# Group 1's input in four 8-row tiles, 16 rows of group 0 scaled on GpSimd, and coefficients three steps later

## Chip, core and metric

The kernel runs on one NeuronCore of one Trainium2 chip. The metric is the device time of one execution in microseconds; the median of three runs is given. Engines are named as in the profile: PE (TensorE, PEld its weight loads), DVE (VectorE), ACT (ScalarE), POOL (GpSimd) and SP (SyncE, which here only issues DMAs; SPq is its queue).

## What is computed

The input x has shape (32, 48, 64, 128): batch, channels, height, width, in fp32. Two layers of the same form are applied:

```
x = x + scan(groupnorm(x, 16 groups), weights of layer 0)
x = x + scan(groupnorm(x, 16 groups), weights of layer 1)

step:   nxt = inp + conv1d(carry, w, K=5 over the line, 48 -> 48 channels) + b
down:   over the rows 0..63, carry = the row above
up:     over the rows 62..0, same weights
right:  over the columns 0..127, right weights
left:   over the columns 126..0, left weights
```

Group normalization takes mean and variance over 3 channels x 64 x 128 of each image, with eps 1e-5 and no learned factors. Every scan step needs the one before it.

## The kernel before

**Groups and phases.** The batch is cut into four groups of 8 images (0 to 3). `PHASES` is the order of work: rows of group 0, rows of group 1, columns of groups 0 and 1 together, then rows of group 2, rows of layer 1, and so on: 12 phases. A row phase has 126 steps (63 down, 63 up), a column phase 254. A step (`step`, line 647) is nine matmuls into three PSUM tiles (line 658) and three VectorE additions of PSUM, bias and input, in place in SBUF (line 667). Steps are counted through the whole kernel: step 0 is the first of group 0's rows, step 126 the first of group 1's.

**Layout.** For a row phase the 64 rows of a group lie in two of three SBUF slots, half of the rows in each; a slot is six units of 128 x 2048. `arena` holds the three slots and four more units, `stage`. The channels and eight columns share the partitions, in three blocks (o = 0, 1, 2).

**How a group gets in.** `plan_input` plans it for groups 1 to 3. `take_in` loads rows of x into a tile (`nat`), half of the rows on partitions 0 to 47 and half on 64 to 111. In the kernel before, group 1's tiles hold 16 rows and there are two (`nats1`), which take turns over four loads; a tile of 8 rows or more per half is loaded image by image with `take_batch`, 192 KB each. `permute` (line 499, GpSimd) reorders a tile into two 8 KB-per-partition tiles in `stage`, 16 copies for each 8 rows. `put_out` stores them to the DRAM tensor `xin`, in DMAs of 384 KB. `take_others` makes the statistics on ScalarE: for each image and each 512 elements a sum (line 364), a negation for all of them together (line 372), and a sum of squares about the mean (line 356). `scaling`, spread over the steps by `spread` at one piece a step, turns them into scale and offset for each channel and image; its first VectorE instructions are lines 382 (needs the sums) and 387 (needs the squares). It ends with `coeffs`, 14 steps after its start.

**How rows get into a scan.** `plan_rows` plans, by step, `move_rows` (loads `xin` into the slots, or stores results to `upa`; 10 DMAs for 8 rows and 20 for 16, in pieces of 128 bytes) and `scale_rows` (ScalarE applies scale and offset in place, line 542, 24 activations for each call). `scale_at_once` (line 546) does the same with two tensor_tensor operations on an engine of choice (line 553); before, only VectorE used it, for group 0's rows 0 to 3. Group 0 is fed by `first_group`, written out by hand; its rows 40 to 63 are scaled by `scale_rows` at steps 10, 26 and 32.

**What sets the order.** `at(t, ...)` puts a call on an agenda for step t; the agenda is sorted and emitted between the steps. `in_order` keeps the emitted order on every engine and queue. A planned step is thus a place in each engine's program, not a time: an engine or a queue can run ahead of the steps or behind them. Within one engine nothing overtakes: a VectorE instruction that waits holds up all the additions behind it, and a DMA on SP's queue that waits holds up every later one. Each DMA also waits for the DMA eight places before it.

The places around the change: group 1's row loads at steps 92, 108, 128 and 144 (`ahead`), its scaling at 112, 124, 143 and 159 (`scaled`), the stores of group 0's rows 56 to 63 at 94, then 8 rows each at 102, 110 and 118.

Of the kernel before, what the change touches and what calls it, by code (L numbers as in the profile page):

```python
# [91 lines left out]
def kernel(  # L92
# [8 lines left out]
    nc = tc.nc  # L101
# [8 lines left out]
    UNIT = NH * LINE  # L110
    SLOT = 2 * NG * UNIT
# [147 lines left out]
    def stat_tile(shape, name, key):  # L259
        return stat_pool.tile(shape, F32, tag=name, name=f"{name}_{key}")  # L260

    def scaling(key, layer, g, averages, masks):


        n = len(masks)
        yield from averages(key)
        mean_p, var_p = averages.result

        def average(ps, rhs):
            for i in range(n):  # L270
                nc.tensor.matmul(ps, masks[i], rhs[:, i], start=i == 0, stop=i == n - 1)

        def expand(ps, rhs):
            for o in range(NG):
                nc.tensor.matmul(ps[:, o], maskp[:, o], rhs, start=True, stop=True)

        def small(name):
            return stat_tile([FULL, NG, GB], name, key)

        ps = ps_stat.tile([FULL, 2 * NG + 2, GB], F32, tag="ps_stat", name=f"ps_{key}")  # L280
        average(ps[0:P, 0], mean_p)
        yield
        mean_c = stat_tile([P, GB], "mean_c", key)
        nc.vector.tensor_copy(mean_c, ps[0:P, 0])
        yield
        expand(ps[:, 1 : 1 + NG], mean_c)
        yield
        mean = small("mean")
        nc.vector.tensor_copy(mean, ps[:, 1 : 1 + NG])
        at = mean if n > 1 else mean_c.unsqueeze(1)  # L290
        np_ = FULL if n > 1 else P
        spare = small("dev")
        dev = spare[0:np_, 0:n]
        nc.vector.tensor_tensor(dev, mean_p, at, ALU.subtract)
        nc.vector.tensor_tensor(dev, dev, dev, ALU.mult)
        nc.vector.tensor_tensor(dev, dev, var_p, ALU.add)
        yield
        average(ps[0:P, 1 + NG], dev)
        yield
        var_c = stat_tile([P, GB], "var_c", key)  # L300
        nc.vector.tensor_copy(var_c, ps[0:P, 1 + NG])
        yield
        expand(ps[:, 2 + NG :], var_c)
        yield
        var = small("var")
        nc.vector.tensor_scalar(var, ps[:, 2 + NG :], GN_EPS, None, ALU.add)

        std = small("std")
        nc.scalar.activation(std, var, AF.Sqrt)
        yield  # L310
        yield
        r0 = std
        nc.vector.reciprocal(r0, std)
        t0 = spare
        nc.vector.tensor_tensor(t0, var, r0, ALU.mult)
        nc.vector.tensor_tensor(t0, t0, r0, ALU.mult)
        yield
        nc.vector.tensor_scalar(t0, t0, -0.5, 1.5, ALU.mult, ALU.add)
        scale, offset = (
            stat_pool.tile(  # L320
                [FULL, NG, GB], F32, tag=f"{t}{layer}{g}", name=f"{t}{layer}{g}"
            )
            for t in ("scale", "offset")
        )
        nc.vector.tensor_tensor(scale, r0, t0, ALU.mult)
        nc.vector.scalar_tensor_tensor(offset, mean, -1.0, scale, ALU.mult, ALU.mult)
        coeffs[layer, g] = scale, offset
# [140 lines left out]
    x_masks = [mask_sb]  # L468
# [45 lines left out]
    def row(k, h):  # L514
        return row_views(k)[h // HALF][:, :, h % HALF]
# [221 lines left out]
    def at(t, fn, *args):  # L737
        agenda.append((t, len(agenda), fn, args))

    def spread(t, gen, every):  # L740


        def go(t):
            if next(gen, "end") != "end":
                at(t + every, go, t + every)
                agenda.sort(key=lambda a: a[:2])

        at(t, go, t)

    def plan_input(g, times, work, lag, nats, perms):  # L750

        stats = InputStats(f"x{g}", 0)
        rows = nats[0].shape[-1] // W
        ahead, pieces_of = len(nats), rows * W // BN
        per = rows * W * GB // perms[0].shape[-1]
        for j, t in enumerate(times):
            nat = nats[j % ahead]
            if j == 0 and g > 1:
                at(t - 7, take_in, g, 0, nat)
            for i in range(per):  # L760
                perm, r = perms[i % len(perms)], i * rows // per
                at(t + i * work / per, permute, nat, r, perm, [nc.gpsimd])
                at(t + i * work / per + 4, put_out, g, 2 * rows * j + r, perm, rows)
            at(t + lag, stats.take_others, pieces_of * j, nat)
            if j + ahead < len(times):
                free = t + (13.5 if g == 1 else 7)
                at(free, take_in, g, 2 * rows * (j + ahead), nat)
        spread(t + work + lag + (0, 3, 8, 5)[g], scaling(f"x{g}", 0, g, stats, x_masks), 1)

    def plan_rows(k, t0, prev):  # L770
        if k == 1:
            ahead, scaled = (-34, -18, 2, 18), (-14, -2, 17, 33)
        elif prev == "cols":
            ahead, scaled = (-28, -12, 4, 20), (-13, 3, 19, 35)
        else:
            ahead, scaled = (-54, -43, 0, 11), (-22, -8, 16, 30)
        if k:
            for i in range(4):
                at(t0 + ahead[i], move_rows, k, i * LOAD, (i + 1) * LOAD, False)
                at(t0 + scaled[i], scale_rows, k, i * LOAD, (i + 1) * LOAD)  # L780

        cuts = list(range(0, H + 1, E8))
        following = PHASES[k + 1][0] == "cols"
        if following and follows(k + 1):
            cuts = [0, E8 // 4] + cuts[1:]
        for h0, h1 in zip(cuts, cuts[1:]):
            t = t0 + 2 * (H - 1) - h0
            if k == 0:
                t += 24 if h0 >= HALF else 68
            elif not following:  # L790
                t = t0 + 92 + 5 * (H - h1) / E8 + (34 if h1 <= HALF else 0)
            at(t, move_rows, k, h0, h1, True)
        at(
            t0 + H - 1,
            nc.gpsimd.tensor_copy,
            last.rearrange("p (o n) -> p o n", o=NG),
            row(k, H - 1),
        )

    def follows(k):  # L800

        _, layer, pair = PHASES[k]
        return PHASES[k - 1] == ("rows", layer, 2 * pair + 1)
# [104 lines left out]
    starts = [0]  # L908
# [5 lines left out]
    def wide_nat(i0, n):  # L914
        return arena[0:P, i0 : i0 + GB * n * W].rearrange("p (b m) -> p b m", b=GB)

    tiles = [stage[0:P, i] for i in range(4)]
    nats1 = [wide_nat(2 * SLOT + i * UNIT * 4, 8) for i in range(2)]
    plan_input(1, [starts[0] + 38 + 13 * j for j in range(4)], 11, 2, nats1, tiles[2:4])
    nats = [wide_nat(3 * SLOT, 4)]  # L920
    times = [starts[2] + 16 + 13.5 * j for j in range(8)]
    plan_input(2, times, 6, 6, nats, tiles[2:4])
    times = [t + 15 * j for t in (starts[3] + 42, starts[4] + 24) for j in range(4)]
    plan_input(3, times, 6, 7, nats, tiles[2:4])

    def more_weights(key, layer, way):
# [135 lines left out]

    in_order(first_group)
    at(starts[0] + 10, scale_rows, 0, 40, 48)
    at(starts[0] + 22, take_in, 1, 16, nats1[1])
    at(starts[0] + 26, scale_rows, 0, 48, 56)
    at(starts[0] + 32, scale_rows, 0, 56, 64)

    agenda.sort(key=lambda a: a[:2])
    done = 0  # L1070
# [65 lines left out]
```

## Time and profile before

| what | value |
|---|---|
| median of three runs | 4380.13 us (4379.56 to 4392.25) |
| profiled execution | 4375.56 us, span of the core 4373.8 us |
| mean granted TensorE clock | 0.98 |
| busy: PE / DVE / ACT / POOL | 95% / 49% / 31% / 19% |
| loads of x for group 1 | 64 DMAs of 192 KB |
| loads of x for groups 2 and 3 | 32 DMAs of 768 KB, median 12.1 us from issue to landing |
| stores to `xin` for groups 1 to 3 | 96 DMAs of 384 KB, median 5.5 us |

Times in a timeline are us from the span's start; a line gives start, length, engine, source line, operation, out<-in, number of merged instructions, and in brackets the idle time before it and what ended that. The span is the profiled core's own time; the execution's time is 1.8 us longer. A busy share is an average over the whole span, so it says little about a single stage.

### The profile page before, as it was taken

Reading aid. Unit: us, or ns where it says so; the run is one execution under the profiler, and the core shown is the slowest. Engines: PE = TensorE matmul, PEld = TensorE weight load, DVE = VectorE, ACT = ScalarE, POOL = GpSimd, SP = SyncE. Lnnn points to the kernel's source line nnn. Section 1 sums busy time; section 2 is a strip of 40 time slices with the busy share of each in tenths; the row PEclk is TensorE's granted clock in tenths of the full one; section 3 lists DMA queues with packets and bytes.
Section 4 is the critical chain, followed back from the end, with each engine's and each line's share of the span. In section 5 each row is a group of like instructions: output and inputs, shape, how many; then the busy total and the mean of one; then the engine's idle time right before and its main releaser. Section 6 shows DMA issues by size and latency. Waiting matters only on the chain. (4 is left out here: it accounts for less than half of the span.)

```text
span 4373.8 us, 90099 instructions
## 1 busy us (share of the span) xinstructions
PE 4149.4 (95%) x36632; PEld 4120.7 (94%) x36632; DVE 2164.2 (49%) x6558; ACT 1360.7 (31%) x2698; POOL 820.4 (19%) x775
## 2 busy tenths in 40 slices
PE   5889997999999999998999999999999999999992
PEld 2889997999999999998999999999999999999992
DVE  6344443456665444443446665444444444444443
ACT  2783301434785554100005774503000002110122
POOL 4351000324332020000004310000000024510352
PEclk9999998999999999999999999999999999999996
DMA  9989789866999989579407989939188039989999
GB/s 194 176 171 154 116 149 183 225 120 189 235 195 147 155 156 158 99 124 209 77 1 222 224 174 143 134 51 165 35 141 189 1 76 240 245 239 159 168 196 182
DMA packets 2111167, 680.34 MB, mean 156 GB/s; under 512 B 2000928, under 2 KB 2053920, under 8 KB 2070816
## 3 DMA queue, kind: packets, MB, share of 16 engines
q1 hardware_dynamic: 2010496, 576.00, 69.7%
q10 hardware_dynamic: 100256, 98.59, 10.8%
q8 instruction: 288, 4.72, 0.5%
q14 instruction: 127, 1.04, 0.1%
HBM read 397.57 MB, written 295.98 MB: 159 GB/s over the span
## 5 line engine op out<-in xcount | busy, mean ns | idle before, releaser
L542 ACT ACTIVATE arena<-arena,offset,scale 128x256 f32<-128x256 f32 (+2 forms) x864 | 601.2, 790 | 412.4 <-DVE arena L667 142.4
L595 POOL TENSOR_TENSOR arena<-arena 128x2048 f32<-128x2048 f32 x80 | 363.0, 4553 | 1660.0 <-PE step_01l L658 504.4
L499 POOL COPY arena<-arena 112x256 f32<-112x256 f32 x458 | 270.3, 646 | 753.7 <-DMA arena<-in_x 504.1
L433 ACT ACTIVATE early<-arena 128x256 f32<-128x256 f32 x192 | 129.5, 675 | 687.5 <-DMA arena<-xin 547.4
L658 PE MATMUL step_00r<-arena,early 128*128 128x128 f32 x2286 | 258.6, 277 | 22.6 <-DMA arena<-upa 22.6
L658 PEld LDWEIGHTS step_00r<-arena,early 128*128 128x128 f32 x2286 | 258.4, 194 | 22.9 <-issue 22.8
L658 PE MATMUL step_01r<-arena,early 128*128 128x128 f32 x2286 | 257.4, 276 | 20.1 <-DMA arena<-upa 20.1
L658 PEld LDWEIGHTS step_01r<-arena,early 128*128 128x128 f32 x2286 | 257.1, 193 | 20.4 <-issue 20.3
L364 ACT ACTIVATE early<-arena 112x512 f32<-112x512 f32 x192 | 121.0, 630 | 460.5 <-PE step_00r L658 246.6
L658 PE MATMUL step_11r<-arena,early 128*128 128x128 f32 x2286 | 258.9, 277 | 3.9 <-DVE arena L667 3.9
L658 PEld LDWEIGHTS step_11r<-arena,early 128*128 128x128 f32 x2286 | 258.2, 193 | 4.4 <-DVE arena L667 4.2
L658 PE MATMUL step_00l<-arena,wleft 128*128 128x128 f32 x2286 | 256.3, 275 | 0.0
L658 PE MATMUL step_10r<-arena,early 128*128 128x128 f32 x2286 | 256.0, 275 | 0.0
L658 PEld LDWEIGHTS step_10r<-arena,early 128*128 128x128 f32 x2286 | 255.7, 192 | 0.3
L658 PEld LDWEIGHTS step_00l<-arena,wleft 128*128 128x128 f32 x2286 | 255.7, 192 | 0.0
L658 PE MATMUL step_11l<-arena,wleft 128*128 128x128 f32 x2286 | 255.5, 275 | 0.0
L658 PE MATMUL step_10l<-arena,wleft 128*128 128x128 f32 x2286 | 255.5, 275 | 0.0
L658 PE MATMUL step_01l<-arena,wleft 128*128 128x128 f32 x2286 | 255.4, 275 | 0.0
L658 PEld LDWEIGHTS step_10l<-arena,wleft 128*128 128x128 f32 x2286 | 255.4, 192 | 0.0
L658 PEld LDWEIGHTS step_11l<-arena,wleft 128*128 128x128 f32 x2286 | 255.4, 192 | 0.0
L658 PEld LDWEIGHTS step_01l<-arena,wleft 128*128 128x128 f32 x2286 | 255.3, 192 | 0.0
L620 ACT COPY arena<-arena 128x256 f32<-128x256 f32 x172 | 99.5, 657 | 415.5 <-POOL arena L595 127.5
(175 smaller groups left out, 7043.9 us busy)
## 6 DMA issues: line engine op xcount, KB each, us to landing
xin<-arena SPq DMA_DIRECT2D x96, 384.0 KB, 5.5
arena<-xin SPq DMA_DIRECT2D x96, 384.0 KB, 8.1
mid<-arena SPq DMA_DIRECT2D x96, 384.0 KB, 7.8
arena<-mid SPq DMA_DIRECT2D x192, 192.0 KB, 4.4
upb<-arena SPq DMA_DIRECT2D x192, 192.0 KB, 3.9
arena<-upb SPq DMA_DIRECT2D x96, 384.0 KB, 11.8
arena<-xin SPq DMA_DIRECT2D x186, 192.0 KB, 4.3
upa<-arena SPq DMA_DIRECT2D x180, 192.0 KB, 3.9
```

The lines of the kernel that those rows point to most:

```text
L364: nc.scalar.activation(junk[0:P], piece, AF.Identity, accum_out=self.sum[:, at[0], at[1]],)
L433: nc.scalar.activation(junk[:, 0:n], view[:, b], AF.Identity, accum_out=self.sum[:, i, j : j + 1])
L499: copy(dst[:, r, q], src[:, r0 + r, q])
L542: nc.scalar.activation(args[0], args[0], AF.Identity, bias=args[2], scale=args[1])
L595: eng.tensor_tensor(unit, unit, nat, ALU.add)
L620: copy(by_w(perm)[:, a], src[:, a])
L658: nc.tensor.matmul(part(whole(ps[o]), -s), weights[:, i, FULL * (o - NG * s - i + 1) : FULL * (o - NG * s - i + 2)], part(src(i), s), star ...
```

## The change

Group 1's input goes through four tiles of 8 rows in place of two of 16, in the same memory. With 4 rows per half, `take_in` uses its other branch: one DMA of 768 KB for each half in place of eight of 192 KB. The tiles are planned at steps 46, 52, ... 88 (before: 38, 51, 64, 77), each permuted over 5 steps, with statistics 1 step after; a tile is reloaded 7 steps after its start (before: 13.5). The first four loads are emitted at the end of `first_group` and at steps 23, 24 and 25; before, the second one was at step 22.

Rows 48 to 55 and 56 to 63 of group 0 are scaled by GpSimd with `scale_at_once`, at steps 26 and 33, in place of ScalarE at steps 26 and 32. On GpSimd these four operations stand between its last permute of group 0 and its first of group 1.

The start of group 1's `scaling` is last tile + work + lag + an extra: before 77 + 11 + 2 + 3 = 93, after 88 + 5 + 1 + 2 = 96. The scaling of group 1's first 16 rows moves from step 112 to 114.

On SP's queue the order after is: eight loads of x, then four times (four stores, two loads), then twelve stores, the loads of group 1's rows 0 to 15, and the last tile's four stores, two ahead of group 0's first eight result rows and two behind them. No stored, loaded or computed element is added or left out.

```diff
         def plan_input(g, times, work, lag, nats, perms):
             ...
             if j + ahead < len(times):
-                free = t + (13.5 if g == 1 else 7)
+                free = t + 7
                 at(free, take_in, g, 2 * rows * (j + ahead), nat)
-        spread(t + work + lag + (0, 3, 8, 5)[g], scaling(f"x{g}", 0, g, stats, x_masks), 1)
+        spread(t + work + lag + (0, 2, 8, 5)[g], scaling(f"x{g}", 0, g, stats, x_masks), 1)
 
     def plan_rows(k, t0, prev):
         if k == 1:
-            ahead, scaled = (-34, -18, 2, 18), (-14, -2, 17, 33)
+            ahead, scaled = (-34, -18, 2, 18), (-12, -2, 17, 33)
         ...
-    nats1 = [wide_nat(2 * SLOT + i * UNIT * 4, 8) for i in range(2)]
-    plan_input(1, [starts[0] + 38 + 13 * j for j in range(4)], 11, 2, nats1, tiles[2:4])
+    nats1 = [wide_nat(2 * SLOT + i * UNIT * 2, 4) for i in range(4)]
+    plan_input(1, [starts[0] + 46 + 6 * j for j in range(8)], 5, 1, nats1, tiles[2:4])
     ...
     in_order(first_group)
     at(starts[0] + 10, scale_rows, 0, 40, 48)
-    at(starts[0] + 22, take_in, 1, 16, nats1[1])
-    at(starts[0] + 26, scale_rows, 0, 48, 56)
-    at(starts[0] + 32, scale_rows, 0, 56, 64)
+    for j in range(1, 4):
+        at(starts[0] + 22 + j, take_in, 1, 8 * j, nats1[j])
+    at(starts[0] + 26, scale_at_once, 0, 48, 56, nc.gpsimd)
+    at(starts[0] + 33, scale_at_once, 0, 56, 64, nc.gpsimd)
```

## The prediction

> **What bounds the kernel now.** I read the page's table of busy time and its slices first, then windows, then the timelines of the engines in the windows with a hole.
>
> ```profile
> PE 4149.4 (95%) x36632; PEld 4120.7 (94%) x36632; DVE 2164.2 (49%) x6558; ACT 1360.7 (31%) x2698; POOL 820.4 (19%) x775
> PE   5889997999999999998999999999999999999992
> PEclk9999998999999999999999999999999999999996
> ```
>
> TensorE works 95% of the span. A slice is 109 us: after the first seven the row of digits is almost all 9. The 2,024 steps (eight row phases of 126, four column phases of 254) are a serial chain of nine matmuls and three VectorE additions, 2.015 us a step, that no part of the change touches. So a gain can only come from holes in the first 700 us. Windows of 10 us (columns: length, busy PE, PEld, DVE, ACT, POOL, granted clock, DMA share, GB/s) show the largest, and a smaller one later:
>
> ```profile
> 300.00:310.00 10.00, 9.03 (x81) 8.83 (x80) 3.84 (x12) 5.71 (x16) 0.00 (x0) 1.00 1.05 166
> 310.00:320.00 10.00, 2.23 (x10) 2.24 (x11) 2.03 (x6) 9.56 (x27) 5.50 (x10) 0.71 0.51 164
> 320.00:330.00 10.00, 1.55 (x10) 1.36 (x8) 0.07 (x1) 9.54 (x24) 8.68 (x16) 0.67 0.67 157
> 330.00:340.00 10.00, 8.63 (x63) 8.64 (x64) 5.68 (x18) 0.00 (x0) 8.80 (x16) 0.77 0.67 158
> 460.00:470.00 10.00, 2.94 (x19) 2.51 (x19) 1.03 (x3) 10.00 (x15) 0.00 (x0) 0.72 1.09 165
> ```
>
> ScalarE is full while TensorE stands. The VectorE timeline says what it stands for:
>
> ```profile
> 316.13 0.22 DVE L382 TENSOR_REDUCE mean_x_x<-sum_x_x 112x8 f32<-112x64 f32 x1 [8.73 <-ACT early L364]
> 329.93 0.55 DVE L387 TENSOR_TENSOR neg_x_x<-neg_x_x,mean_x_x 112x64 f32<-112x64 f32 x1 [11.70 <-ACT early L356]
> 468.19 0.35 DVE L667 SCALAR_TENSOR_TENSOR arena<-step_01d,bd,arena 128x128 f32<-128x128 f32 x1 [8.28 <-DMA arena<-xin]
> ```
>
> L382 and L387 compute group 1's coefficients. They stand in VectorE's program order ahead of the additions (L667) of steps 94 and 95, and wait for ScalarE's last sums (L364) and squares (L356). The third is row 32 of group 1's scan, waiting for its scaled input. TensorE's own idle there is 8.74, 9.81 and 7.06 us. What stands behind ScalarE and the DMAs is in the timelines of ScalarE, GpSimd and SP's queue:
>
> ```profile
> 169.29 48.01 ACT L542 ACTIVATE arena<-arena,offset,scale 128x128 f32<-128x128 f32 x94 [2.33 <-DMA arena<-xin]
> 220.52 9.42 POOL L499 COPY arena<-arena 112x256 f32<-112x256 f32 x16 [66.96 <-DMA arena<-in_x]
> 314.50 9.32 POOL L499 COPY arena<-arena 112x256 f32<-112x256 f32 x16 [16.35 <-DMA xin<-arena]
> 196.72 33.20 SPq L199 DMA_DIRECT2D arena<-in_x  x32
> 304.05 41.85 SPq L199 DMA_DIRECT2D xin<-arena  x16
> 345.99 22.36 SPq L199 DMA_DIRECT2D arena<-xin  x20
> 430.18 39.96 SPq L199 DMA_DIRECT2D arena<-xin  x40
> L595 POOL TENSOR_TENSOR arena<-arena 128x2048 f32<-128x2048 f32 x80 | 363.0, 4553 | 1660.0 <-PE step_01l L658 504.4
> ```
>
> ScalarE scales until 217.3 and only then takes statistics, 25.9 us per 16-row tile (16 sums at 0.755, one negation, 16 squares at 0.846). GpSimd is free from 153.6 to 220.5. SP needs 149.3 us (196.72 to 345.99) for group 1's pass. At the rates seen (loads of x at 165 GB/s, 12.6 MB; the stores at about 380 GB/s, 12.6 MB) it is 76 + 33 = 109 us; 40 us are waits between load, permute and store.
>
> **What the Trainium skill says.** "GPSIMD Engine Reference", Elementwise — side-by-side cycle accounting, gives 4497 ns for a GpSimd tensor_tensor of 2048 fp32; L595 above agrees with 4553. The same page, Specifications, says that the two engines share SBUF ports and contend when VectorE has two SBUF inputs. L667 has one and one from PSUM; its minimum, median and maximum here are 340, 350 and 354 ns, with GpSimd busy or not, so I charge nothing. "TensorE: Matmul & The Clock Gate", What's actually happening, says that idleness of some 3.4 us halves the clock until it has been busy as long. Here the clock is 0.67 to 0.77 around the holes, and the nine matmuls after one took 3.8 us instead of 2.0: a hole costs some 1.8 us beyond itself. "DMA: Bandwidth & Descriptors", Measured (HBM→SBUF), has larger transfers run faster. For x this trace doesn't: a 768 KB pair of group 2, alone, moved 143 to 244 GB/s between 872 and 879 us, no better than the 192 KB loads. I take 165 GB/s for both.
>
> **The change part by part.**
>
> Scaling on GpSimd. ScalarE loses 48 of its 168 128x128 activations (0.51 us each): free at 169.3 + 46 x 0.51 = 192.8. GpSimd gains four operations of 128 x 3072. At 4553/2048 = 2.22 ns per element each is 6.8 us, 13.7 for 8 rows. (VectorE's L553 with the same broadcast took 1.14 ns an element, its plain L595 1.12, so broadcasting is free there.) Rows 48 to 55 land at about 190.8 (SP issues them by 186.5, 4.3 us to landing): done at 204.5. Rows 56 to 63: done at 218.1. VectorE's last addition of the down scan is at 244.7, so they are needed at 214.5 and 230.6. Slack 10 and 12.5 us: no cost, while one operation stays under 10 us. Queued behind are GpSimd's permutes, which started at 220.5 anyway. Bounds: 5 us each (nothing gained) to 14 (16 us lost).
>
> Four tiles. SP issues eight loads at 196.7, as many bytes as before; after some 4 us of backlog a tile lands every 9.5 us: 210.5, 220, 229.5, 239. ScalarE needs 13.05 us a tile: 210.5 + 8 x 13.05 = 314.9, its last sums at 308. Tiles 4 to 7 must not starve it. SP's order is four stores, two loads, and so on. Tile 0's stores wait behind the loads and land at 243; from there load plus stores take 9.5 + 4.2 = 13.7: tiles 4 to 7 land at 253, 266, 280, 294, and ScalarE wants them at 263, 276, 289, 302. After that GpSimd's 4.7 us half permutes and 5.5 us landings set the pace: tile 6's last permute ends at about 316, and SP reaches group 1's first row loads at about 317 instead of 345.99, 29 us earlier. Tile 7's four stores (4.2 us) come after those loads, which read other rows.
>
> Coefficients three steps later (start 96, not 93). L382 comes after step 96: TensorE stopped at 309.0 after step 93, so at 315; ScalarE's sums are there from 308. L387 comes at 318; the squares from 314.9. Both waits vanish. Step 95 ended at 335.18; without waits 309.0 + 4.0 = 313.0: 22.1 us. Those small VectorE operations now stand between steps instead of in the hole: about 2 us back. **Net 20 us.** The scaling of rows 0 to 15 also moves two steps. Coefficients are ready near 345, ScalarE takes 18 us, group 1's scan starts near 377: nothing, 14 us of slack cover it.
>
> What is late next. TensorE would reach row 32 of group 1 at 461.5 - 20 - 1.2 (a short wait at row 16, which goes) = 440.3. SP's loads for it start 88.4 us after its first row loads (84.2 before, plus tile 7's stores), 405.4 instead of 430.18; the rest is unchanged, so row 32 goes on at 468.6 - 24.8 = 443.8. A wait of 3.5 us stays, and the gain is what the DMA stream gains: **24.8 us**. The holes at 129, 174 and 660 us keep their causes.
>
> Against the profiled execution, 4375.56 us (span 4373.8), that is 4350.8. The median of the three runs is 4.6 above it: 4380.1 - 24.8 = **4355**.
>
> **Rivals.**
> - The stream is faster than priced (tile cycle 13 instead of 13.7, or the 40 us of waits shrink further). Then TensorE arrives last and all holes close: 20 + 1.2 + 7.1 + 1.8 = 30: 4350. For: the waits were large. Against: DMA share is already 1.05 there.
> - The stream is slower: a lone pair of large loads trailed off for 2 us at a low DMA share (880 to 882 us); 1.5 us for each of eight tiles puts the row loads at 329, and row 32 has the gain of 12.8: 4367. For: GpSimd's two permute tiles still wait for landings.
> - ScalarE stays last: tile 0 lands 5 us later, L387 waits 2 us. Row 32's wait absorbs it; same end, 4355.
> - Slower: GpSimd's broadcast multiply-add is the bound. Row 56 waits 190.8 + 4p - 230.6 for p us an operation; beyond 30 us (p over 17.5) it eats all that TensorE could gain. At p = 20: 4391. Only 2.6 times the priced row would do it; no row here shows this view on GpSimd.
>
> **How the numbers follow.** About 0.3%, 13 us, is what a measurement of this kernel can tell from no change. Forecast or ScalarE last 0.64, faster stream 0.16, slower stream 0.14 (half of it within 13 us), GpSimd slow 0.06 (0.04 slower, 0.02 within). Faster 0.87, same 0.09, slower 0.04. The range takes the fast stream less a few us of run to run spread, and the slow stream with 3 more: 4346 to 4370.
>
> **What would show it.** Right: L553 on POOL near 6.8 us; no wait at L382 and L387; TensorE busy from 310 to 340; SP's first row loads near 317; a wait of 3 to 4 us at row 32, near 444. Wrong: a wait of L667 for POOL near 214 or 230; row loads not before 330; a longer hole at row 32, which would mean that the scan only ran ahead of its input.

## The result and the profile after

The changed kernel takes 4359.91 us (median of six runs, 4345.14 to 4366.88), the kernel before 4381.08 in the same comparison (six runs, 4379.56 to 4392.25). The ratio is 0.9948, 95% interval 0.9936 to 0.9960: 23 us less by the ratio, 18 to 28 by the interval (the medians differ by 21.2). The forecast was 4355, 24.8 us less. One execution of those below is left out of every ratio: 10296.8 us, of the kernel before with later coefficients, more than twice any other.

The page of the changed kernel, the same three rows as before:

```profile
PE 4146.8 (95%) x36632; PEld 4118.3 (95%) x36632; DVE 2164.3 (50%) x6558; ACT 1336.8 (31%) x2654; POOL 847.6 (19%) x779
PE   4899998999999999998999999999999999999993
PEclk9999999999999999999999999999999999999996
```

The third digit of the PE row (218 to 327 us), where the first hole of the kernel before begins, is 9 instead of 8. The seventh (654 to 763 us), the hole before the columns, is 8 instead of 7, and the 8 of the clock row in the same place is gone. One thing must be known before times are compared: the profiled span is 4358.0 us, only 15.8 less than before. In this execution the first matmul of step 0 began at 101.86 us, in the one before at 94.78, with the same program up to there; over all the traces below it lies between 94.78 and 102.95. It is spread that the change does not make, so **from here on the text counts times from the first matmul of step 0** and calls it the scan's start. Lines of a profile keep their own clock.

Windows of the changed kernel (length, busy PE, PEld, DVE, ACT, POOL, granted clock, DMA share, GB/s):

```profile
310.00:320.00 10.00, 10.00 (x92) 10.00 (x91) 4.88 (x16) 9.55 (x28) 8.87 (x16) 1.00 0.46 105
320.00:330.00 10.00, 8.77 (x78) 8.58 (x78) 6.45 (x21) 3.10 (x8) 8.88 (x16) 1.00 0.62 149
330.00:340.00 10.00, 10.00 (x92) 10.00 (x92) 5.39 (x19) 0.00 (x0) 9.55 (x17) 1.00 0.96 172
450.00:460.00 10.00, 5.43 (x46) 5.01 (x45) 2.48 (x8) 10.00 (x15) 0.00 (x0) 0.99 1.07 153
```

The first hole has shrunk to 1.23 us. The VectorE timeline has the instructions of the old waits, and a new wait at row 16 (418.91) ahead of the one at row 32:

```profile
319.84 0.21 DVE L382 TENSOR_REDUCE mean_x_x<-sum_x_x 112x8 f32<-112x64 f32 x1
323.23 0.60 DVE L387 TENSOR_TENSOR neg_x_x<-neg_x_x,mean_x_x 112x64 f32<-112x64 f32 x1 [1.29 <-ACT early L356]
418.91 0.35 DVE L667 SCALAR_TENSOR_TENSOR arena<-step_01d,bd,arena 128x128 f32<-128x128 f32 x1 [7.22 <-ACT arena L542]
459.05 0.35 DVE L667 SCALAR_TENSOR_TENSOR arena<-step_01d,bd,arena 128x128 f32<-128x128 f32 x1 [5.76 <-ACT arena L542]
```

L382 no longer waits (it has no bracket), L387 for 1.29 us instead of 11.70. TensorE's own idle is 6.01 us at row 16, where it was about 1, and 4.55 at row 32, where it was 7.06. Its lines at row 32 and at the first column step, of the kernel before:

```profile
468.60 65.57 PE L658 MATMUL step_01d<-arena,early 128*128 128x128 f32 x558 [7.06 <-DVE arena L667]
683.45 36.79 PE L658 MATMUL step_00r<-arena,early 128*128 128x128 f32 x301 [22.63 <-DMA arena<-upa]
```

and of the changed kernel, with row 16 ahead of them:

```profile
419.32 35.59 PE L658 MATMUL step_01d<-arena,early 128*128 128x128 f32 x288 [6.01 <-DVE arena L667]
459.45 0.53 PE L658 MATMUL step_01d<-arena,early 128*128 128x128 f32 x2 [4.55 <-DVE arena L667]
460.19 63.77 PE L658 MATMUL step_01d<-arena,early 128*128 128x128 f32 x556 [0.21 <-DVE arena L667]
671.19 48.98 PE L658 MATMUL step_00r<-arena,early 128*128 128x128 f32 x421 [20.59 <-DMA arena<-upa]
```

In the changed kernel two matmuls of row 32 come ahead of one more short wait; "row 32 goes on" below means the longer run behind it (460.19). The timelines of ScalarE, GpSimd and SP's queue:

```profile
218.28 0.63 ACT L364 ACTIVATE early<-arena 112x512 f32<-112x512 f32 x1 [18.30 <-DMA arena<-in_x]
203.87 6.70 POOL L553 TENSOR_TENSOR arena<-arena,scale 128x3072 f32<-128x3072 f32 x1 [45.25 <-DMA arena<-xin]
252.28 9.47 POOL L499 COPY arena<-arena 112x256 f32<-112x256 f32 x16 [12.08 <-DMA xin<-arena]
308.41 9.43 POOL L499 COPY arena<-arena 112x256 f32<-112x256 f32 x16 [5.87 <-DMA xin<-arena]
203.44 18.08 SPq L199 DMA_DIRECT2D arena<-in_x  x8
330.19 21.38 SPq L199 DMA_DIRECT2D arena<-xin  x20
379.87 21.52 SPq L199 DMA_DIRECT2D arena<-xin  x20
420.83 40.43 SPq L199 DMA_DIRECT2D arena<-xin  x40
```

SP reaches group 1's first row loads at 330.19, which is 228.3 from the scan's start; before it was 251.2. That is the gain, on its way. ScalarE's waiting for its first tile (18.30) is not on TensorE's path, as the version below shows in which ScalarE gets its scaling back. GpSimd's waits for stores to land belong to the turn of load, permute and store that leads to these row loads. Step by step:

| from the scan's start, us | before | after | difference | forecast |
|---|---|---|---|---|
| SP's loads of rows 0-15 begin | 251.2 | 228.3 | -22.9 | -29 |
| SP's loads of rows 32-47 begin | 335.4 | 319.0 | -16.4 | -24.8 |
| row 32 goes on | 373.8 | 358.3 | -15.5 | -24.8 |
| first column step (group pair 0) | 588.7 | 569.3 | -19.4 | -24.8 |
| end of the span | 4279.0 | 4256.1 | -22.9 | -24.8 |

Between row 32 and the first column step it gains 3.9 us more: the hole before the columns is 20.59 us instead of 22.63, the kernel before ran at a lower clock behind its longer hole (0.77 from 470 to 480 us; the changed kernel had 0.84 from 460 to 470), and 0.7 us are the two matmuls that row 32 had ahead. The last matmul of all ends 18.4 us earlier (4199.2 and 4180.8 from the scan's start). The other 4.5 us of the 22.9 come behind it, where the last results are written: that stretch took 79.9 us before and 75.4 after, and between 74.6 and 81.7 over the eleven traces of this text, in no order of the versions. So they cannot be put down to the change.

### The profile page after: what moved, and what is told of

Read it like the earlier page. It is cut to its first block, busy times and chain, and to the rows that moved or that the text cites. A ratio compares the mean times of both kernels' runs of the same rounds, so it can differ in the third digit from the quotient of the medians.

```text
span 4358.0 us, 89939 instructions
## 1 busy us (share of the span) xinstructions
PE 4146.8 (95%) x36632; PEld 4118.3 (95%) x36632; DVE 2164.3 (50%) x6558; ACT 1336.8 (31%) x2654; POOL 847.6 (19%) x779
## 5 line engine op out<-in xcount | busy, mean ns | idle before, releaser
L542 ACT ACTIVATE arena<-arena,offset,scale 128x256 f32<-128x256 f32 (+2 forms) x816 | 576.5, 799 | 400.7 <-DMA arena<-mid 198.2
L595 POOL TENSOR_TENSOR arena<-arena 128x2048 f32<-128x2048 f32 x80 | 363.0, 4552 | 1662.2 <-PE step_01l L658 505.7
```

What stands on the lines that cost most here:

```text
L542: nc.scalar.activation(args[0], args[0], AF.Identity, bias=args[2], scale=args[1])
L595: eng.tensor_tensor(unit, unit, nat, ALU.add)
```

## The experiments

Two theories were set against each other. **Stream**: SP's queue, with everything that stands on it in order, decides when the rows 32 to 47 of group 1 are there; holes of TensorE before that are only places where it waits for the same thing. **Holes**: each wait of VectorE or ScalarE that is taken away is won by itself. (In the changed kernel the DMA engines are not full just ahead of the row loads, where the queue waits for GpSimd's last permutes: shares of 0.46 and 0.62 in the windows above. From the row loads on they are: 0.96 and 1.07.)

### The kernel before, coefficients later and nothing else

```diff
-        spread(t + work + lag + (0, 3, 8, 5)[g], ...
+        spread(t + work + lag + (0, 13, 8, 5)[g], ...
-            ahead, scaled = (-34, -18, 2, 18), (-14, -2, 17, 33)
+            ahead, scaled = (-34, -18, 2, 18), (-8, -2, 17, 33)
```

> The kernel before, with only the coefficients moved: start at step 103 instead of 93, the first 16 rows of group 1 scaled at step 118 instead of 112. Two tiles, ScalarE scales all rows. Stream theory: the waits at L382 and L387 go (22 us of idle and slow clock), but SP's row loads stay at 251 us from the first matmul, so group 1's scan waits for rows 0 and 1 (some 12 us), row 16 and row 32, and row 32 goes on at 374 as before: total within 4 us of the kernel before, 4377 to 4384. Rival (VectorE's wait for the coefficients was the bound): 4360, as fast as the changed kernel.

Measured: 4376.67 us (twenty runs) against 4377.13, ratio 1.0001 (0.9993 to 1.0008). The trace is of another run of the same version:

> The kernel before with the coefficients ten steps later, for its trace (its times were on a par with the kernel before, 1.0001). Stream theory: no wait at L382 and L387; SP's row loads at about 251 us from the first matmul; TensorE waits for rows 0 and 1, 16 and 32 instead, and row 32 goes on at about 374. Rival: row 32 goes on earlier and the time is lost later.

That run took 4378.28 us. VectorE, TensorE and SP's queue in its timelines:

```profile
332.50 0.48 DVE L387 TENSOR_TENSOR neg_x_x<-neg_x_x,mean_x_x 112x64 f32<-112x64 f32 x1 [0.80 <-ACT early L356]
389.51 34.74 PE L658 MATMUL step_01d<-arena,early 128*128 128x128 f32 x288 [13.26 <-ACT arena L542]
429.80 35.20 PE L658 MATMUL step_01d<-arena,early 128*128 128x128 f32 x288 [5.55 <-issue]
469.81 65.82 PE L658 MATMUL step_01d<-arena,early 128*128 128x128 f32 x558 [4.82 <-DVE arena L667]
349.25 22.44 SPq L199 DMA_DIRECT2D arena<-xin  x20
```

The waits at L382 and L387 are as good as gone (0.80 us), and nothing is won. TensorE now stands 13.26 us at the start of group 1's scan, 5.55 at row 16, 4.82 at row 32. The first of these was not made by moving the coefficients: they are there at 359.1, and ScalarE's first scaling of group 1 starts at 369.04, after a wait of 16.18 us for a load of rows. SP's row loads begin at 250.5 as before (251.2), and row 32 goes on at 371.0 (before: 373.8). The largest hole of the profile was worth nothing as long as the stream stood where it was.

### The changed kernel, coefficients back at step 93

```diff
-        spread(t + work + lag + (0, 2, 8, 5)[g], ...
+        spread(t + work + lag + (0, -1, 8, 5)[g], ...
```

> The changed kernel with the coefficients started at step 93 as before, the scaling of rows 0-15 left at step 114. L382 and L387 are again ahead of ScalarE: L387 at about 215 us from the first matmul, the squares at 221, so some 6 us of waiting and 2 us of slow clock. Stream theory: rows 16 and 32 waited 6.0 and 4.8 us, so they absorb it: 4358 to 4363, as the changed kernel. Rival (the three steps are what pays): 4367.

Measured: 4363.69 us, ratio 0.9960 (0.9945 to 0.9975), not told apart from the changed kernel's 0.9948. VectorE and TensorE:

```profile
320.17 0.45 DVE L387 TENSOR_TENSOR neg_x_x<-neg_x_x,mean_x_x 112x64 f32<-112x64 f32 x1 [5.62 <-ACT early L356]
457.87 64.32 PE L658 MATMUL step_01d<-arena,early 128*128 128x128 f32 x558 [7.79 <-DVE arena L667]
```

The wait at L387 is back, and TensorE no longer waits at row 16; row 32 goes on at 357.4 from the scan's start (changed kernel: 358.3). The wait has moved, the end has not.

### The changed kernel, ScalarE scales rows 48 to 63

```diff
-    at(starts[0] + 26, scale_at_once, 0, 48, 56, nc.gpsimd)
-    at(starts[0] + 33, scale_at_once, 0, 56, 64, nc.gpsimd)
+    at(starts[0] + 26, scale_rows, 0, 48, 56)
+    at(starts[0] + 32, scale_rows, 0, 56, 64)
```

> The changed kernel, but ScalarE scales group 0's rows 48-63 (at steps 26 and 32, as before the change); GpSimd doesn't. ScalarE is free 24.5 us later, which eats the 18 us it had waited for the first tile and 6 more; its squares end some 7 us later, so L387 waits about 8 us instead of 1.3. Stream theory: SP's queue is not later by more than 2 us (GpSimd's permutes start earlier), rows 16 and 32 absorb the wait: total within 3 us of the changed kernel, 4358 to 4363. Rival (ScalarE's chain is what the change relieved): 8 us or more slower, 4368 and up.

Measured: 4360.95 us, ratio 0.9959 (0.9946 to 0.9972). L387 waits 5.02 us, row 32 goes on at 359.1. Moving 25 us of work off ScalarE is worth nothing that can be measured in this place.

### The changed kernel, GpSimd's scaling cut by block

```diff
-        for t, op in zip(coeffs[layer, g], (ALU.mult, ALU.add)):
-            ...
-            eng.tensor_tensor(view, view, t, op)
+        for o in range(NG):                      # on GpSimd
+            for t, op in zip(coeffs[layer, g], (ALU.mult, ALU.add)):
+                ...
+                eng.tensor_tensor(view[:, o : o + 1], view[:, o : o + 1], t, op)
```

> GpSimd's scaling cut by block: three pairs of 128 x 1024 operations for each 8 rows instead of one pair of 128 x 3072. The uncut operation on rows 48-55 started at 102.0 us from the first matmul, 6 us later than forecast, when rows 56-63 were landing too: its range of addresses spans part of them. Theory (a wait for rows 56-63 through the range): cut, it starts near 96, and the permutes of group 1 near 123 instead of 129. Whether that matters: the DMA stream theory says no, since the first four tiles keep the DMA engines full until 147 in any case; SP's row loads stay at 228 and the total at 4360 within 3. Rival (GpSimd's late start made the row loads 6 us later than forecast): row loads at 222, total 4354.

Measured: 4358.84 us, ratio 0.9951 (0.9936 to 0.9966). GpSimd and SP's queue:

```profile
183.95 2.37 POOL L557 TENSOR_TENSOR arena<-arena,scale 128x1024 f32<-128x1024 f32 x1 [29.11 <-DMA arena<-xin]
244.30 9.46 POOL L499 COPY arena<-arena 112x256 f32<-112x256 f32 x16 [22.37 <-DMA xin<-arena]
322.25 21.82 SPq L199 DMA_DIRECT2D arena<-xin  x20
```

Cut by block (L557 is the former L553), the first operation starts at 85.7 from the scan's start, not at the 96 expected: a block needs three or four of the ten loads. The uncut one started at 102.0. GpSimd is free 14.6 us earlier, and then waits 22.37 us, instead of 12.08, for the first stores to land. The row loads begin at 224.0; traces whose programs agree with the changed kernel up to there (coefficients at step 93, and the three versions with another order on SP's queue, below) lie at 224.5 to 226.6, the changed kernel itself at 228.3. That is 4.3 us after the cut version in the changed kernel's own trace and 0.5 to 2.6 us in the other four. So GpSimd's late start explains at most a part of the 6 us that the forecast was off, and the time doesn't show it.

### The changed kernel, loads image by image

```diff
-            if n < E8:
+            if n < E8 and g != 1:
```

With this, group 1's tiles take the branch of `take_batch`: 96 KB for each DMA, with the same 2 KB runs.

> Group 1's four tiles loaded image by image: 16 DMAs of 96 KB for each tile instead of two of 768 KB; the contiguous runs in DRAM stay 2 KB. In the changed kernel the first four tiles moved at some 150 GB/s (10.4 us a tile), against 165 in the kernel before with 4 KB runs and 192 KB DMAs; I had taken 165 for both. If the run length sets the rate: still about 150, first four tiles done at 147 us from the first matmul, total 4357 to 4364. If the large DMA's form costs it: about 165, four tiles done at 142, row loads some 5 us earlier, total 4355. If large transfers carry the gain: the many issues hold SP back, the row loads are 5 us or more later, 4366 and up.

Measured: 4361.79 us, ratio 0.9958 (0.9943 to 0.9972). A window of the changed kernel in which only loads of x run, one after the stores have begun, and a window of this kernel with loads alone:

```profile
221.00:224.00 3.00, 3.00 (x30) 3.00 (x29) 1.31 (x4) 2.63 (x9) 3.00 (x1) 1.00 1.07 152
248.00:251.00 3.00, 3.00 (x29) 3.00 (x28) 1.57 (x5) 2.87 (x9) 0.00 (x0) 1.00 1.06 337
```

```profile
215.00:225.00 10.00, 10.00 (x92) 10.00 (x91) 4.80 (x15) 9.54 (x25) 9.92 (x2) 1.00 0.92 163
```

The large DMAs moved 152 GB/s with the engines full, the small ones 163 at a share of 0.92. It is no chance of these windows: over the seven traces with 768 KB loads, windows of 5 us between 210 and 225 us have 141 to 156 GB/s. The second permute waits for the first tile's stores, which stand behind the first four tiles' loads on SP's queue. It starts at 143.8 from the scan's start (changed kernel: 150.4; six other traces with 768 KB loads: 145.9 to 149.0). But 16 issues for each tile take SP some 11 us, the cycle is 16 us a tile instead of 14, and the row loads begin at 228.4. Run length did not set the rate. The large transfers bring nothing here. "DMA: Bandwidth & Descriptors" of the Trainium skill, Measured (HBM→SBUF, 128 partitions, SWDGE, issued from GpSimd), has larger transfers run faster; for these loads, with 48 partitions and issued from SP, it is the other way round, and the measurement decides.

### The four tiles alone

Three of the parts undone together: loads image by image, ScalarE scales rows 48 to 63, coefficients at step 93 and rows 0 to 15 scaled at step 112.

> The four tiles of 8 rows alone: loads image by image (96 KB), ScalarE scales rows 48-63, coefficients at step 93, rows 0-15 scaled at step 112. What is left of the change is the finer turn of the tiles. Stream theory: SP's row loads still come at 225 to 229 us from the first matmul instead of 251; L387 waits some 12 us, rows 16 and 32 less in exchange; total within 5 us of the changed kernel, 4358 to 4367. Rival (the parts are needed together): 4370 and up.

Measured: 4363.70 us, ratio 0.9955 (0.9941 to 0.9970). TensorE and SP's queue:

```profile
324.28 4.21 PE L658 MATMUL step_00u<-arena,early 128*128 128x128 f32 x18 [7.26 <-DVE arena L667]
331.37 3.19 PE L658 MATMUL step_00u<-arena,early 128*128 128x128 f32 x18 [2.88 <-DVE arena L667]
461.78 0.49 PE L658 MATMUL step_01d<-arena,early 128*128 128x128 f32 x2 [2.09 <-DVE arena L667]
329.77 22.09 SPq L199 DMA_DIRECT2D arena<-xin  x20
```

About 10 us of idle at L382 and L387 are back, the wait at row 16 is gone and the one at row 32 has shrunk to 2.09. SP's row loads begin at 226.8. The time is that of the whole change, as far as these intervals tell.

What is left of the change is the finer turn of the tiles and one thing more, which no run takes apart from it: the last tile's four stores stand behind the row loads of rows 0 to 15, where in the kernel before all stores stood ahead of them. GpSimd's permutes of the last tile, in the changed kernel:

```profile
329.57 4.74 POOL L499 COPY arena<-arena 112x256 f32<-112x256 f32 x8 [1.11 <-DMA xin<-arena]
334.75 4.73 POOL L499 COPY arena<-arena 112x256 f32<-112x256 f32 x8 [0.45 <-POOL arena L499]
```

They end at 339.48, 9.3 us after the row loads began. In the kernel before, the row loads began 0.95 us after the end of the last permute (345.04 and 345.99). With the last stores ahead of them they would thus begin some 10 us later in the changed kernel, of which the 3.5 us that these stores take behind them would come back for the later rows. This is an estimate from these figures: up to 10 of the 22.9 us at the row loads, and some 7 of the 16.4 at rows 32 to 47, can be the stores' place and not the smaller tiles.

### Order on SP's queue: row loads before result stores

```diff
-            ahead, scaled = (-34, -18, 2, 18), (-12, -2, 17, 33)
+            ahead, scaled = (-34, -33, 2, 18), (-12, -2, 17, 33)
```

> Loads of group 1's rows 16-31 put directly behind those of rows 0-15 on SP's queue, ahead of group 0's result stores. Times count from the first matmul of step 0 (changed kernel: row 16 goes on at 317.5 after 6.0 us of idle, row 32 at 358.3 after 4.8 us). Stream theory (the end is set by when SP's queue, full of bytes, reaches the loads of rows 32-47): the 6 us at row 16 go, row 32's loads start where they did, row 32 still goes on at 358 with about 11 us of idle before it: total the same within 3 us, about 4360. Rival (each hole of TensorE counts by itself): row 32 goes on 6 to 8 us earlier, total about 4353.

Measured: 4357.49 us, ratio 0.9955 (0.9940 to 0.9971). The ten runs lie between 4343.65 and 4370.34, so the times alone can't choose between 4360 and 4353; the trace can. TensorE and SP's queue:

```profile
451.51 65.63 PE L658 MATMUL step_01d<-arena,early 128*128 128x128 f32 x558 [14.01 <-DVE arena L667]
322.59 20.07 SPq L199 DMA_DIRECT2D arena<-xin  x20
344.42 23.38 SPq L199 DMA_DIRECT2D arena<-xin  x20
412.31 39.82 SPq L199 DMA_DIRECT2D arena<-xin  x40
```

The 6 us at row 16 are gone and row 32 waits 14.01 us, one hole instead of two. Rows 32 to 47 begin to load at 315.1 from the scan's start, 89.7 after the first row loads (changed kernel: 90.6), and row 32 goes on at 354.3. It is 4 us earlier than in the changed kernel's trace, and the whole row stream is 3 us earlier there.

### The same, and rows 48 to 63 of group 0 stored later

```diff
             if k == 0:
                 t += 24 if h0 >= HALF else 68
+                if h0 >= 48:
+                    t = 129 + (h0 == 48)
```

> As the order variant, and group 0's rows 48-63 are stored after the loads of rows 32-47 instead of before (they share no place with them; rows 32-47 are still stored first). Same bytes. Stream theory: 20 DMAs of some 20 us leave the front of the loads of rows 32-47, so these start some 20 us earlier and neither row 16 nor row 32 waits: 6.0 + 4.8 us of idle and about 2 us of slow clock go, total 4347 (4343 to 4352). Row 48 becomes the next candidate, up to 3 us. Rival (the stores are needed early, or the hole moves to row 48): total 4357 to 4362.

Measured: **4346.37 us** (four runs, 4344.39 to 4350.94), ratio 0.9925 (0.9902 to 0.9949). TensorE and SP's queue:

```profile
186.08 64.34 PE L658 MATMUL step_00d<-arena,early 128*128 128x128 f32 x558 [3.81 <-DVE arena L667]
654.76 105.49 PE L658 MATMUL step_00r<-arena,early 128*128 128x128 f32 x917 [21.39 <-DMA arena<-upa]
396.56 20.55 SPq L199 DMA_DIRECT2D arena<-xin  x20
417.16 19.20 SPq L199 DMA_DIRECT2D upa<-arena  x20
436.41 21.17 SPq L199 DMA_DIRECT2D arena<-xin  x20
```

Between row 32 of group 0 and the first column step the list of TensorE's waits is empty. Rows 32 to 47 begin to load at 294.8 from the scan's start instead of 319.0, with the same bytes in another order, and the first column step comes at 553.0 instead of 569.3. By the medians of that comparison it takes 31 us less than the kernel before. Against the changed kernel, measured in another series, the intervals of the ratios still overlap (0.9925, 0.9902 to 0.9949, and 0.9948, 0.9936 to 0.9960); it is the trace that shows the gain. Of the 16.3 us at the first column step, 11.0 are left at the last matmul (4169.8 against 4180.8). Where the others go is open.

### The same, coefficients back at step 93

> The version with group 0's rows 48-63 stored later (4346), with the coefficients back at step 93. There no later wait of TensorE is left to absorb the wait at L387: some 5.5 us and 2 us of slow clock should now be paid in full: 4352 to 4355. Rival (the steps' place makes no difference): 4346.

Measured: 4352.72 us (four runs, 4348.69 to 4353.76), ratio 0.9929 (0.9913 to 0.9946). L387 waits again:

```profile
319.48 0.67 DVE L387 TENSOR_TENSOR neg_x_x<-neg_x_x,mean_x_x 112x64 f32<-112x64 f32 x1 [4.93 <-ACT early L356]
```

The first column step comes at 561.7 from the scan's start, 8.7 later than without; 7.6 of that arise after the turn of group 0's row scan, where L382 and L387 stand. The median is 6.4 us later, but the two versions were compared in different series, and their ratios overlap: the trace shows the wait to be paid here, the times alone do not. The same three steps were worth nothing in the changed kernel.

## Why the prediction was right, and where its sums were off

- **What bounds it, and what is late next: right.** The forecast made the gain equal to what SP's row stream gains, not to the 22 us of holes at L382 and L387. The kernel before with later coefficients (1.0001), and three undone parts that changed nothing, show it. The last version but one shows it from the other side: with the queue in another order rows 32 to 47 load 24.2 us earlier (3.6 of them by an earlier start of the stream in that trace), and TensorE no longer waits for any row of group 1.
- **Scaling on GpSimd, at no cost: right.** An operation took 6.70 to 6.74 us against 6.8 estimated, and no row waited. It began 6 us later than worked out. Cutting it by block frees it; that the range of addresses of the uncut one made it wait for rows 56 to 63 fits this, and is argued only. What the part brings was worked out as part of ScalarE's chain; undone, the time is the same.
- **Four tiles: right in kind, off in size.** The load rate was taken too high. I took 165 GB/s for 768 KB DMAs, 9.5 us a tile; with the engines full they moved some 150, which is 10.5 us, about 4 us over the first four tiles. The lone pair of group 2 that I read it from is no measure: it averaged 180 GB/s from 872 to 879 us, more than the 192 KB loads and not "no better". Yet the second permute, forecast at 148.2 from the scan's start (243), came at 150.4, and at 145.9 to 149.0 in six other traces with these loads. What is late in all seven comes behind it: from the second permute to the row loads 74 us were forecast, 77.9 came (76.5 to 79.5 in the other six). Of these 3.9 us, 1.3 are four turns of 14.0 us instead of 13.7 (the second tile's permute starts at 252.28, the sixth's at 308.41) and 2.6 the end, from the sixth tile's permute to the row loads: 21.8 instead of 19.2, where GpSimd's last permutes set the pace. The row loads began 23 us earlier in the changed kernel's trace, and 25 to 27 in four others; 29 was forecast.
- **The wait at row 16 "which goes": wrong.** Before, TensorE came to row 16 at 427.6 and went on at 429.3. By the forecast's own terms the input would have been there at 429.3 - 24.8 = 404.5 and TensorE at 427.6 - 20 = 407.6, some 3 us of slack. With the stream 6.1 us later, 49.7 us instead of 47.6 (43.4 before, plus 4.2 for the last tile's stores) between the two row loads, and TensorE there 1.4 us earlier, it became a wait of 6.0 us. By the stream theory it costs nothing by itself, and the order variant, which removes it, shows that.
- **Row 32: off by 9 us in the trace pair** (15.5 instead of 24.8 earlier): 6.1 from the stream's start, 2.2 from the way to rows 32 to 47 (90.6 instead of 88.4), 1.0 from landing and scaling (39.4 instead of 38.4, of which 0.7 are the short wait behind two matmuls). Later gains of 7.4 us, of which I foresaw none, bring the end to 22.9, and 4.5 of them are the spread of the last stretch. So part of the nearness of 4355 to 4359.9 is luck.
- **Coefficients, net 20 us: right, but not what pays.** Group 1's first addition came 21.4 us earlier from the scan's start (301.9 to 280.5).
- **The rivals.** The slow stream (4367) and the fast one (4350) bracket what came. In none of these traces did a row wait for GpSimd's scaling.

Open: how much of the gain the smaller tiles bring and how much the new place of the last tile's stores; what makes the stream's start differ by 4 us between traces of one program; and what in the form of the 768 KB loads makes them slower than the 96 KB ones.

## What to carry to other kernels

When an engine's chain and a DMA queue both feed the same later point, follow the queue to that point first: here the largest hole, closed ahead of it, only moved there. A part that is worth nothing can become worth several microseconds once the later wait is gone, as the three steps of the coefficients did by the traces, so undo the parts again after the bound has moved. The order of loads and stores on a full queue is a resource: storing late what nothing waits for brought the first column step from 567.9 to 553.0, 15 us, without moving a byte less.

## What the runs showed of the hardware beyond expectation

- Large DMAs were the slower ones for x: 152 GB/s at 768 KB against 163 at 96 KB, both with 2 KB runs and 48 partitions.
- A GpSimd multiply or add with a broadcast operand costs no more than a plain one: 6.70 us for 3072 elements is 2.18 ns an element, against 2.22 for L595.
- Up to the first scan step the same program took 94.8 to 103.0 us over eleven traces, about as much as a third of the change's gain.
